# Denominators and theta in one two-bank score tile, with the key chunks around them

## The chip, the cores and the metric

The kernel runs on one core of one Trainium2 chip. Its time is that of one execution on the device in microseconds (us), the median of several runs. Engines are named as the profile does: PE (TensorE matmuls), PEld (TensorE weight loads, which can run beside matmuls), DVE (VectorE), ACT (ScalarE), POOL (GpSimd), SP (SyncE, which here only triggers transfers). Work of the core is in fp32 throughout.

## The reference

Two non-local attention layers are applied one after the other to an image batch of 4 x 128 channels x 96 x 96. Cut to what matters, a layer is:

```python
g_x     = maxpool2(conv1x1(x, g_w, g_b))        # 64 x 2304 keys: the values
theta_x = conv1x1(x, theta_w, theta_b)          # 64 x 9216 queries
phi_x   = maxpool2(conv1x1(x, phi_w, phi_b))    # 64 x 2304 keys
f = einsum('bqc,bck->bqk', theta_x, phi_x)
y = einsum('bqk,bkc->bqc', softmax(f), g_x)
out = batchnorm(conv1x1(y, W_w, W_b)) + x       # 128 channels again
```

The batch norm uses stored statistics, so it folds into the weights W and one shift.

## The kernel before

There are 8 blocks (4 images x 2 layers, `ORDER` interleaves the images so that layer 2 of one image runs after layer 1 of another). A block has 9216 queries, worked on as 9 *pairs* of 2 x 512 queries, and 2304 keys, worked on as 18 key tiles of 128.

For one pair and one key tile, `scores` (L238) writes four 64x64 matmuls into a score tile `sc` of 128 x 1024 floats, which is two PSUM banks; ACT turns it into `exp` (L244), with a constant shift in place of the row maximum, and DVE adds it into `sum` (L250). `values` (L258) multiplies `exp` with the values into `av`, which gathers over all 18 key tiles. The loop over `t` emits two key tiles of `scores`, then the two `values` of the step before: nine steps make a pair.

PSUM has three pools: `ps_sc`, two score tiles of two banks; `ps_av`, one tile of two banks; `ps_misc`, two tiles of one bank. Everything else goes through `ps_misc`:

- `denominators` (L270): a matmul of ones with `sum` of the *previous* pair; ACT copies it to `rc` (L275). `normalise` (L278 to L285, DVE) then takes the reciprocal and multiplies.
- `theta` (L227): the queries of the *next* pair; ACT adds the bias on the way out (L232).
- `pooled` (L168, a *chunk* of keys): g and phi of 384 pixels for the *next* block, of which DVE takes the 2x2 maximum into `gphi` (L172). A block needs 24 chunks, three in each of its predecessor's first eight pairs.
- `spread` (L186 to L199): after 8, 16 and 24 chunks, the phi half is centred and copied by ACT, and the g half is transposed by PE. They stand in pairs 3, 6 and 8.
- `project` (L294, L300): the output projection of the previous pair, four steps after the window.

All of these but the last stand in one place of a pair, which the text calls the *window*: after the first `values` of the pair (`j == J_WINDOW`, step 0), in the order

```python
if q: pairs[q - 1].denominators()
for step in others[:1]: step()          # chunk
if q + 1 < len(pairs): pairs[q + 1].theta()
for step in others[1:]: step()          # chunk, chunk, perhaps a spread
if q: pairs[q - 1].normalise()
```

A tile pool gives its buffers out in turn: a tile waits until the readers of the one that had its buffer before are done.

The order on PE, DVE and ACT in this loop is the order of the code: it stands inside `tc.manual_schedule(engines=...)`, where each engine named issues its instructions as written. What lies ahead of the loop is outside of it, and its order is the scheduler's: the loads of x on the queue of SP; the parameters of both layers (`load_layer`, L109 to L149), whose loads are triggered from ACT's queue; the fold of the batch norm (a square root on ACT, L135, then DVE); the transposes of the weights on PE (`transposed`, L102); all 24 chunks and three spreads of the first block; and theta of the first pair. `load_layer` triggers `var` (L133), takes the square root of it (L135) and then triggers `W_nat` (L145).

Of the kernel before, what the change touches and what calls it, by code (L numbers as in the profile page):

```python
# [9 lines left out]
F32 = mybir.dt.float32  # L10
# [6 lines left out]
P = 128  # L17
# [3 lines left out]
QT = 512  # L21
# [11 lines left out]
PT = 2 * QT  # L33
NP = HW // PT
KB = 2
NB = NKT // KB
J_WINDOW, J_PROJECT = 0, 4
# [7 lines left out]
def shifted_blocks(ctx: ExitStack, tc: tile.TileContext, x: bass.AP, layers, out: bass.AP, flag):  # L45
# [23 lines left out]
    ps_sc = ctx.enter_context(tc.tile_pool(name="ps_sc", bufs=2, space=PSUM))  # L69
    ps_av = ctx.enter_context(tc.tile_pool(name="ps_av", bufs=1, space=PSUM))  # L70
    ps_misc = ctx.enter_context(tc.tile_pool(name="ps_misc", bufs=2, space=PSUM))

    ident = const.tile([P, P], F32, name="ident")
    make_identity(nc, ident)
# [9 lines left out]
    def load_x(b):  # L84
        xt = xp.tile([C, HW], F32, tag="x", name=f"x_{b}")
        src = x[b].rearrange("c h w -> c (h w)")
        n = 6
        for i in range(n):
            nc.sync.dma_start(out=xt[:, ts(i, HW // n)], in_=src[:, ts(i, HW // n)])
        return xt  # L90
# [125 lines left out]
    class Pair:  # L216
# [4 lines left out]
            self.name = f"{blk.name}_{p}"  # L221
            self.es = {}

        def theta(self):
            ps = ps_misc.tile([P, QT], F32, tag="misc", name=f"theta_ps_{self.name}")
            for h in range(2):
                nc.tensor.matmul(  # L227
                    ps[ts(h, CI), :], lhsT=self.blk.w["theta"],
                    rhs=self.blk.xt[:, ts(2 * self.p + h, QT)], start=True, stop=True,
                )  # L230
            self.th = work.tile([P, QT], F32, tag="theta", name=f"theta_{self.name}")
            nc.scalar.activation(self.th, ps, AF.Identity, bias=self.blk.w["theta_b"])  # L232
# [31 lines left out]
                self.halves = work.tile([P, PT], F32, tag="halves", name=f"halves_{self.name}", bufs=1)  # L264
                nc.scalar.copy(self.halves, self.av)  # L265

        def denominators(self):
            ps = ps_misc.tile([P, QT], F32, tag="misc", name=f"den_ps_{self.name}")
            for h in range(2):
                nc.tensor.matmul(  # L270
                    ps[ts(h, CI), :], lhsT=ones, rhs=self.sum[:, ts(h, QT)],
                    start=True, stop=True,
                )
            self.rc = work.tile([P, QT], F32, tag="rc", name=f"rc_{self.name}", bufs=1)
            nc.scalar.copy(self.rc, ps)  # L275
# [34 lines left out]
    blocks = []  # L310
# [4 lines left out]
    def begin(n):  # L315

        b, l = ORDER[n]
        if b not in xs:
            xs[b] = load_x(b)
        blocks[n].xt = xs[b]  # L320
        blocks[n].begin_keys()

    begin(0)
    steps = blocks[0].key_steps()
# [2 lines left out]
            step()  # L327

    pairs = [Pair(blk, p, n * NP + p) for n, blk in enumerate(blocks) for p in range(NP)]
    pairs[0].theta()  # L330
    total = len(pairs) * NB
    engines = {mybir.EngineType.PE, mybir.EngineType.DVE, mybir.EngineType.Activation}
    with tc.manual_schedule(engines=engines):
        for t in range(total + NB):
            if t < total:
                q, j = divmod(t, NB)
                if q % NP == 0 and j == 0 and q // NP + 1 < len(blocks):
                    begin(q // NP + 1)
                    steps = blocks[q // NP + 1].key_steps()
                for k in range(j * KB, (j + 1) * KB):  # L340
                    pairs[q].scores(k)
            if t == 0:
                continue
            q, j = divmod(t - 1, NB)
            if j == J_PROJECT and q:
                pairs[q - 1].project()
            if t <= total:
                for k in range(j * KB, (j + 1) * KB):
                    pairs[q].values(k)
            if j == J_WINDOW:  # L350
                others = list(steps.pop(q % NP, [])) if q < len(pairs) else []
                if q:
                    pairs[q - 1].denominators()
                for step in others[:1]:
                    step()
                if q + 1 < len(pairs):
                    pairs[q + 1].theta()
                for step in others[1:]:
                    step()
                if q:  # L360
                    pairs[q - 1].normalise()

    bad = const.tile([P, 2], F32, name="bad")
    nc.vector.tensor_reduce(bad[:, 0:1], rmax, AX.X, ALU.max)
# [3 lines left out]
    ps = ps_misc.tile([P, QT], F32, tag="misc", name="bad_ps")  # L368
# [271 lines left out]
def nonlocal_blocks(tc: tile.TileContext, x: bass.AP, layers, out: bass.AP):  # L640
    with tc.tile_pool(name="flag", bufs=1) as pool:
        flag = pool.tile([1, 1], I32, name="flag")
        shifted_blocks(tc, x, layers, out, flag)
        bad = tc.nc.values_load(flag[0:1, 0:1])
        with tc.If(bad > 0):
            general_blocks(tc, x, layers, out)
# [30 lines left out]
```

## Time and profile before

| | |
|---|---|
| time, median of 3 runs | 2666.67 us (2666.65 to 2666.72) |
| span of the profiled execution | 2666.4 us |
| mean granted TensorE clock | 0.998 |
| PE busy | 2607.6 us |
| of it scores (L238) / values (L258) | 1234.2 us / 1228.8 us |
| chunks (L168) / theta (L227) / denominators (L270) / projection (L294) | 160.5 / 77.2 / 77.7 / 75.7 us |
| DVE / ACT busy | 2131.1 us / 1576.9 us |
| first chunk on PE / first scores | 29.86 us / 55.76 us |

A row of the timeline has the start in us, the duration of the merged group, the engine, the line, the operation, the tiles (output <- inputs), the shape, the count, and in brackets how long the engine was idle before and what ended that. An fp32 matmul of the code is two instructions in the trace, so `denominators` and `theta` are four each, and so is a chunk. Durations of neighbouring matmuls overlap, so the distance from one start to the next says what a group cost.

### The profile page before, as it was taken

How to read it: one execution, taken by the hardware profiler on the slowest of the kernel's cores; microseconds unless marked ns; L12 is line 12 of the kernel's file. 1: busy time of each engine (PE TensorE's matmuls, PEld its weight loads, DVE VectorE, ACT ScalarE, POOL GpSimd, SP SyncE). 2: the span in 40 equal slices, each digit the busy share in tenths (PEclk: the TensorE clock that was granted, in tenths of full speed). 3: DMA queues.
4: the chain of work that ended last, by engine and by line, in shares of the span. 5: the costliest groups of instructions: out<-in, count | busy, mean ns of one | idle time of the engine just before them, and what ended most of it. 6: DMA issues, size and time to landing. Idle time of an engine off the chain costs nothing.

```text
span 2666.4 us, 51928 instructions
## 1 busy us (share of the span) xinstructions
PE 2607.6 (98%) x22808; PEld 896.0 (34%) x22808; DVE 2131.1 (80%) x2203; ACT 1576.9 (59%) x1564; POOL 0.7 (0%) x6
## 2 busy tenths in 40 slices
PE   5999999999999999999999999999999999999998
PEld 1333333333333333333333333333333333333332
DVE  3788787888877888787888778888787887888887
ACT  2655665656656656555665666655665656666664
POOL 0000000000000000000000000000000000000000
PEclk9999999999999999999999999999999999999999
DMA  6000000000000000100000000000000000000000
GB/s 218 1 1 1 1 1 1 1 1 1 1 9 17 17 17 12 77 1 1 1 1 11 15 17 17 17 1 1 1 1 1 17 17 9 17 17 17 17 17 26
DMA packets 11690, 41.48 MB, mean 16 GB/s; under 512 B 3392, under 2 KB 3776, under 8 KB 11456
## 3 DMA queue, kind: packets, MB, share of 16 engines
q1 hardware_dynamic: 8640, 37.75, 3.6%
q8 instruction: 180, 2.95, 0.5%
q10 hardware_dynamic: 2816, 0.34, 0.1%
q14 instruction: 54, 0.44, 0.1%
HBM read 19.21 MB, written 18.87 MB: 14 GB/s over the span
## 4 chain that ended last, share of the span: by engine, by line
PE 95%; ACT 3%; DMA 1%; DVE 1%; issue 0%; ACTq 0%
PE sc L238 42%; PE av L258 41%; PE gphi_ps L168 4%; PE theta_ps L227 3%; PE den_ps L270 3%; PE W_ps L294 2%; ACT theta L232 1%; DMA W_nat<-in_L_conv_W_w_dram 0%; ACT exp L244 0%; DVE centre L186 0%; ACT phi L190 0%; DVE gphi L172 0%; ACT phi L193 0%; DMA theta_b<-in_L_conv_theta_b_dram 0%; DMA theta_nat<-in_L_conv_theta_w_dram 0%
## 5 line engine op out<-in xcount | busy, mean ns | idle before, releaser
L244 ACT ACTIVATE exp<-sc,nshift 128x1024 f32<-128x1024 f32 x1296 | 1375.0, 1112 | 805.5 <-PE sc L238 805.3
L250 DVE TENSOR_TENSOR sum<-sum,exp 128x1024 f32<-128x1024 f32 x1152 | 1410.0, 1224 | 233.1 <-ACT exp L244 142.1
L238 PE MATMUL sc<-theta,phi 64*64 64x512 f32 x10368 | 1234.2, 591 | 6.4 <-ACT exp L244 5.1
L258 PE MATMUL av<-exp,gT 64*64 64x512 f32 x10368 | 1228.8, 589 | 0.0
L258 PEld LDWEIGHTS av<-exp,gT 64*64 64x64 f32 x10368 | 396.3, 133 | 716.1 <-issue 695.0
L238 PEld LDWEIGHTS sc<-theta,phi 64*64 64x64 f32 x10368 | 387.8, 133 | 726.4 <-issue 698.2
L282 DVE RECIPROCAL rc<-rc 128x128 f32<-128x128 f32 x288 | 243.4, 907 | 0.0
L172 DVE TENSOR_REDUCE gphi<-gphi_ps 128x96 f32<-128x384 f32 x192 | 107.0, 558 | 124.2 <-PE gphi_ps L168 123.5
L248 DVE TENSOR_TENSOR sum<-exp,exp 128x1024 f32<-128x1024 f32 x72 | 88.2, 1225 | 137.7 <-ACT exp L244 137.7
L168 PE MATMUL gphi_ps<-x,gphiT 128*64 128x384 f32 x768 | 160.5, 502 | 8.9 <-DVE gphi L172 0.7
L300 DVE SCALAR_TENSOR_TENSOR x<-W_ps,shift,x 128x512 f32<-128x512 f32 x144 | 101.0, 743 | 0.5 <-PE W_ps L294 0.5
L275 ACT COPY rc<-den_ps 128x512 f32<-128x512 f32 x72 | 42.2, 587 | 98.3 <-PE den_ps L270 98.3
L265 ACT COPY halves<-av 128x1024 f32<-128x1024 f32 x72 | 72.9, 1012 | 34.4 <-PE av L258 34.4
L232 ACT ACTIVATE theta<-theta_ps,theta_b 128x512 f32<-128x512 f32 x72 | 49.5, 687 | 69.4 <-PE theta_ps L227 69.2
L168 PEld LDWEIGHTS gphi_ps<-x,gphiT 128*64 128x64 f32 x768 | 48.7, 137 | 124.1 <-ACT theta L232 45.2
L227 PE MATMUL theta_ps<-x,thetaT 128*64 128x512 f32 x288 | 77.2, 614 | 3.4 <-ACT rc L275 1.2
L294 PE MATMUL W_ps<-halves,WT 64*64 64x512 f32 x576 | 75.7, 596 | 5.0 <-DVE halves L283 5.0
L270 PE MATMUL den_ps<-sum,ones 128*64 128x512 f32 x288 | 77.7, 618 | 0.0
L283 DVE TENSOR_TENSOR halves<-halves,rc 128x512 f32<-128x512 f32 x72 | 49.8, 692 | 2.5
L280 DVE TENSOR_TENSOR halves<-halves 128x512 f32<-128x512 f32 x72 | 49.1, 682 | 1.6 <-ACT halves L265 1.6
L284 DVE TENSOR_REDUCE rmax<-rc 128x1 f32<-128x512 f32 x72 | 48.9, 678 | 0.0
L285 DVE TENSOR_REDUCE rmin<-rc 128x1 f32<-128x512 f32 x72 | 48.6, 676 | 0.0
(45 smaller groups left out, 153.8 us busy)
## 6 DMA issues: line engine op xcount, KB each, us to landing
x<-in_x_dram SPq DMA_DIRECT2D x24, 768.0 KB, 9.1
out_dram<-x SPq DMA_DIRECT2D x36, 512.0 KB, 2.6
theta_nat<-in_L_conv_theta_w_dram ACTq DMA_DIRECT2D x2, 32.0 KB, 5.2
theta_b<-in_L_conv_theta_b_dram ACTq DMA_DIRECT2D x4, 0.2 KB, 5.9
gphi_nat<-in_L_conv_g_w_dram ACTq DMA_DIRECT2D x2, 32.0 KB, 5.3
gphi_nat<-in_L_conv_phi_w_dram ACTq DMA_DIRECT2D x2, 32.0 KB, 4.9
g_b<-in_L_conv_g_b_dram ACTq DMA_DIRECT2D x2, 32.0 KB, 5.1
W_nat<-in_L_conv_W_w_dram ACTq DMA_DIRECT2D x2, 32.0 KB, 6.8
```

The costliest lines, as they stand in the source:

```text
L168: nc.tensor.matmul(ps[ts(h, CI), :CC], lhsT=self.w["gphi"][:, ts(h, CI)], rhs=self.xt[:, ts(r, CC)], start=True, stop=True,)
L172: nc.vector.tensor_reduce(self.gphi[:, ts(r, CC // 4)].rearrange("p (h w) -> p h w", w=W // 2), ps[:, :CC].rearrange("p (h a w b) -> p h w ...
L227: nc.tensor.matmul(ps[ts(h, CI), :], lhsT=self.blk.w["theta"], rhs=self.blk.xt[:, ts(2 * self.p + h, QT)], start=True, stop=True,)
L238: nc.tensor.matmul(ps[ts(c, CI), ts(h, QT)], lhsT=self.blk.phi[ts(h, CI), ts(2 * k + c, CI)], rhs=self.th[ts(h, CI), :], start=True, stop= ...
L244: nc.scalar.activation(e, ps, AF.Exp, bias=nshift)
L248: nc.vector.tensor_add(self.sum, self.es[0], e)
L250: nc.vector.tensor_add(self.sum, self.sum, e)
L258: nc.tensor.matmul(self.av[ts(h, CI), ts(r, QT)], lhsT=self.blk.gT[ts(r, CI), k, :], rhs=e[ts(r, CI), ts(h, QT)], start=(k == 0), stop=(k ...
L270: nc.tensor.matmul(ps[ts(h, CI), :], lhsT=ones, rhs=self.sum[:, ts(h, QT)], start=True, stop=True,)
L282: nc.vector.reciprocal(rc[:, ts(i, P)], rc[:, ts(i, P)])
L294: nc.tensor.matmul(pss[h][ts(c, CI), :], lhsT=self.blk.w["W"][ts(h, CI), ts(c, CI)], rhs=self.y[ts(h, CI), :], start=True, stop=True,)
L300: nc.vector.scalar_tensor_tensor(dst, pss[h], self.blk.w["shift"], dst, op0=ALU.add, op1=ALU.add)
```

## The change

Denominators and theta no longer take a bank each of `ps_misc`: they get one tile of `ps_sc`, a `room`, whose first 512 columns (one bank) are for the denominators and whose last 512 (the other) are for theta. So the room takes a turn among the score tiles, and `ps_misc` is left to chunks, transposes and projections. In the window two chunks now stand ahead of the pair of them, and the third, with the spread, behind. The point is that no two neighbours in the window should need the same bank.

The region with the written order now begins right behind the pools and holds the whole program of `shifted_blocks`, the opening too.

```diff
@@ -70,6 +70,9 @@
     ps_misc = ctx.enter_context(tc.tile_pool(name="ps_misc", bufs=2, space=PSUM))
 
+    engines = {mybir.EngineType.PE, mybir.EngineType.DVE, mybir.EngineType.Activation}
+    ctx.enter_context(tc.manual_schedule(engines=engines))
+
     ident = const.tile([P, P], F32, name="ident")
...
-        def theta(self):
-            ps = ps_misc.tile([P, QT], F32, tag="misc", name=f"theta_ps_{self.name}")
+        def theta(self, room):
+            ps = room[:, QT:]
...
-        def denominators(self):
-            ps = ps_misc.tile([P, QT], F32, tag="misc", name=f"den_ps_{self.name}")
+        def denominators(self, room):
+            ps = room[:, :QT]
...
-    pairs[0].theta()
+
+    def room(n):
+
+        return ps_sc.tile([P, PT], F32, tag="sc", name=f"den_theta_ps_{n}")
+
+    pairs[0].theta(room(0))
     total = len(pairs) * NB
-    engines = {mybir.EngineType.PE, mybir.EngineType.DVE, mybir.EngineType.Activation}
-    with tc.manual_schedule(engines=engines):
-        for t in range(total + NB):
...
-                if q:
-                    pairs[q - 1].denominators()
-                for step in others[:1]:
-                    step()
-                if q + 1 < len(pairs):
-                    pairs[q + 1].theta()
-                for step in others[1:]:
-                    step()
-                if q:
-                    pairs[q - 1].normalise()
+    for t in range(total + NB):
...
+            for step in others[:2]:
+                step()
+            both = room(q + 1)
+            if q:
+                pairs[q - 1].denominators(both)
+            if q + 1 < len(pairs):
+                pairs[q + 1].theta(both)
+            for step in others[2:]:
+                step()
+            if q:
+                pairs[q - 1].normalise()
```

## The prediction

> **What bounds the kernel now.** I read the page first: busy time by engine, then the chain that ended last.
>
> ```profile
> PE 2607.6 (98%) x22808; PEld 896.0 (34%) x22808; DVE 2131.1 (80%) x2203; ACT 1576.9 (59%) x1564; POOL 0.7 (0%) x6
> ...
> PE 95%; ACT 3%; DMA 1%; DVE 1%; issue 0%; ACTq 0%
> ```
>
> TensorE (PE) is busy 98% of the span and 95% of the chain. But a PE counted as busy may still be losing time, since matmul ends are modelled. So I took starts, not busy times, from the timeline of PE through one window (the work between two score groups of a pair).
>
> ```profile
> 205.07 1.90 PE L258 MATMUL av<-exp,gT 64*64 64x512 f32 x16
> 206.89 1.08 PE L270 MATMUL den_ps<-sum,ones 128*64 128x512 f32 x4
> 207.80 0.82 PE L168 MATMUL gphi_ps<-x,gphiT 128*64 128x384 f32 x4
> 208.66 1.08 PE L227 MATMUL theta_ps<-x,thetaT 128*64 128x512 f32 x4
> 209.57 1.82 PE L168 MATMUL gphi_ps<-x,gphiT 128*64 128x384 f32 x8
> 211.32 1.95 PE L238 MATMUL sc<-theta,phi 64*64 64x512 f32 x16
> ```
>
> Score and value groups start every 1.72 us throughout, so nothing is lost there. In the window, denominators and theta each take 0.91 to the next start (512 columns). A chunk has 384 columns, yet takes 0.86 ahead of theta, and two chunks take 1.75. What should a chunk take? The timeline of the opening, where chunks follow each other, has weight loads at 35.75, 36.40 and 37.27: 0.65 when the bank is free, 0.87 when it is not. In the first window, which has no denominators, chunk (61.93) to theta (62.63) is 0.70. So the window holds waits that no row of idle time shows. The timeline of all engines names them:
>
> ```profile
> 208.02 0.59 ACT L275 COPY rc<-den_ps 128x512 f32<-128x512 f32 x1 [1.39 <-PE den_ps L270]
> 208.66 0.20 PEld L227 LDWEIGHTS theta_ps<-x,thetaT 128*64 128x64 f32 x4 [0.71 <-ACT rc L275]
> ...
> 209.78 0.69 ACT L232 ACTIVATE theta<-theta_ps,theta_b 128x512 f32<-128x512 f32 x1 [1.18 <-PE theta_ps L227]
> ...
> 210.52 0.20 PEld L168 LDWEIGHTS gphi_ps<-x,gphiT 128*64 128x64 f32 x4 [0.81 <-ACT theta L232]
> ```
>
> Theta's weight load starts at 208.66, right after the copy of the denominators ends (208.02+0.59=208.61): third user of two banks. The third chunk's starts at 210.52, right after theta's activation ends (210.47): fifth user. The list of waits counts them:
>
> ```profile
> PEld gphi_ps L168 <- ACT theta L232: 45.2, 56, 0.8
> PEld theta_ps L227 <- ACT rc L275: 41.1, 62, 0.7
> ```
>
> 56 is 7 blocks x 8 windows with three chunks. The microseconds there are idle time of the weight loader, most of it beside running matmuls, and are not the gain.
>
> The opening matters too, because the change orders it. Its timeline:
>
> ```profile
> 19.47 0.45 ACTq L97 DMA_DIRECT2D var<-in_L_conv_bn_var_dram  x1
> ...
> 20.01 0.39 ACTq L145 DMA_DIRECT2D W_nat<-in_L_conv_W_w_dram  x1
> ...
> 27.16 0.29 ACT L135 ACTIVATE std<-var,eps 128x1 f32<-128x1 f32 x1 [12.25 <-DMA W_nat<-in_L_conv_W_w_dram]
> ...
> 29.86 9.80 PE L168 MATMUL gphi_ps<-x,gphiT 128*64 128x384 f32 x40
> ```
>
> These are layer 1's parameters. The load of W_nat is triggered *before* the square root that waits for var, although the code has it after (L135, L145). PE's first chunk follows the transpose of that W, at 29.86.
>
> **What the Trainium skill says.** "TensorE: Matmul & The Clock Gate", Part 2, step 1: matmuls stay in program order and only weight loads are pulled ahead. So a load held by a bank stops all behind it; the trace agrees (210.52). "TensorEngine Tiling (Array Packing)", Key Properties: changing the tiling mode drains the engine. The trace agrees: values to denominators is 1.82, 0.10 over 1.72, and a last chunk to scores 211.32-210.52=0.80, over the 0.65 of chunk to chunk. "PSUM — Partial Sum Buffer", Specifications, gives 512 fp32 values a bank, so a 1024-wide score tile is two banks: denominators have one half, theta the other. Its section on bank collisions asks for guards by bank, so theta's matmul need not wait for the copy of the denominators; no run shows this tile yet.
>
> **The change part by part.**
>
> *No operation is added or removed.* All durations stay; only order and buffers move.
>
> *Windows with three chunks.* New order: chunk, chunk, denominators, theta, chunk. With no wait, from the end of the values: mode change 0.10; chunk to chunk 0.65; chunk to a 512 group 0.70; denominators 0.91 (followed directly by theta in the last block, 2589.19 to 2590.10, also 0.91); theta to chunk 0.91; chunk to scores 0.80. Sum 4.07. Now: 211.32-205.07-1.72=4.53. Gain 0.46.
>
> Can it be free of waits? The third chunk takes the first chunk's bank at 206.79+3.27=210.06 on this window's clock. VectorE is busy with sums until 208.21, then needs 0.56 to reduce: free at about 208.8. The shared tile takes a score slot last read by an exp that ends before the window. The second score tile after it wants that slot back: theta's activation ends 1.81 after theta's start (208.66 to 210.47), call it 1.86 with the signal. The first score tile starts at 0.91+0.80=1.71 and the second 0.86 later, at 2.57. No wait. VectorE's third reduce comes 0.46 earlier with the window, so normalise and the projection keep their distance. Gain: 55 x 0.46 + 0.25 for the first window (3.31 now, 0.65+0.70+0.91+0.80=3.06 then) = 25.5 us.
>
> *Windows without a chunk behind theta*: 8 in the last block, 7 with the last spread. Nothing waits there now. Then the second score tile would start at theta + 0.96 + 0.86 = 1.82, and the slot is free at 1.86, with no weight load ahead. Between 0 and 0.25 each; I take 0.1: 1.5 us given back.
>
> *Spreads after chunks* (14 windows): `others[2:]` keeps them behind the last chunk, and the ScalarE work ahead of the next exp is unchanged, so the 0.7 us waits of scores on exp stay as they are.
>
> *The opening in written order.* With ScalarE ordered from the start, its queue runs W_nat of layer 0 and all of layer 1 behind the first square root (13.3). Twelve triggers then lead to var of layer 1, against eight now. Now the seventh of them (mean, 19.09) waits for the landing of the first (theta_nat, 13.45 to 19.08), six outstanding. The twelfth then waits for the sixth, triggered near 16.2: 16.2+5.5=21.7, against 19.47. Var took 7.7 to the square root (27.16): 29.4. Only now is W_nat triggered, at 29.6 in place of 20.01. It needs 4.3 (layer 0's: 9.08 to 13.3) to 9.2 (layer 1's: 20.01 to 29.2). With 0.66 to the first chunk, PE starts at 34.6 to 39.5, against 29.86. Behind that wait stand all of PE's chunks, and behind them everything. Bounds: 0, if the order of triggers does not move, and 10. The loads of x keep the DMA engines at 0.9 to 1.0 busy until 40 us, so I lean high: +7.5.
>
> Sum: 2666.7 - 25.5 + 1.5 + 7.5 = 2650.2 us.
>
> **The rivals.**
>
> A. The opening does not get longer: triggers keep their places, or W_nat lands in time. For: only the trace's order says that they were moved ahead. Against: the region names the engine whose queue triggers them. 2666.7-24.0=2642.7.
>
> B. Half the window gain is eaten by a wait I do not see, such as the third chunk on a late reduce (VectorE is 80% busy). For: sums run into the window. Against: 1.2 us of margin above. 2666.7-12.7+1.5+7.5=2663.
>
> C. The first score tile behind the window gets the shared slot. It then waits from 1.71 to 1.86 and loses its early weight load (about 0.3 in all) in 56 windows, and 1.86-0.96=0.9 in 15: +30 in place of +1.5. For: slots are not named in the code. Against: the other slot has been free longer. 2666.7-25.5+30+7.5=2679, slower.
>
> D. Theta's matmul is held behind the copy of the denominators because they share a tile: it starts 1.13+0.59+0.05=1.77 behind the denominators, not 0.91; 71 x 0.86=61. Against: dependencies are kept by region elsewhere: five transposes of gphi run at 52.49 while the last chunk's reduce still writes that tile, and only the sixth waits. 2650+61=2711, slower.
>
> **How the numbers follow.** Forecast 0.64, A 0.20, B 0.08, C 0.05, D 0.03. 0.2% is 5.3 us, so faster is under 2661.3. The forecast and A are, and a little of B: 0.87. The rest of B, and a C that nearly cancels: 0.05. C and D: 0.08. Range: A with 2 us of error gives 2640; the forecast with the opening at +10 and 0.2 us more lost in the 15 windows is 2656, and B reaches to 2662. 2640 to 2662 leaves out C and D and a tail of B.
>
> **What would show it.** Right: chunks at 0.65 to 0.70 apart, 4.07 per window, no wait of theta's load on the copy or of a chunk's on theta; chunk one near 37; W_nat's second trigger behind the second square root. Wrong: score loads waiting on theta's activation in 56 windows (C), theta 1.77 behind the denominators (D), chunk loads waiting on a reduce (B), a first chunk still at 30 (A).

## The result, and the profile after

The changed kernel takes 2701.98 us (2701.21 to 2702.55) against 2666.69 us for the kernel before on the same chip: a ratio of 1.0131, 95% interval 1.0114 to 1.0149. It is slower by 1.3%, where 0.6% faster was forecast.

The page of the changed kernel first, busy time by engine and the shares of the chain that ended last:

```profile
PE 2596.6 (96%) x22808; PEld 899.0 (33%) x22808; DVE 2122.1 (79%) x2203; ACT 1577.9 (58%) x1564; POOL 0.7 (0%) x6
...
PE 95%; ACT 3%; DMA 1%; DVE 1%; issue 0%; ACTq 0%
```

PE is busy for 11 us *less* (it was 2607.6) in a span 34 us longer: work has not grown, idle time has. The timeline of PE in the window that answers to the one shown of before:

```profile
212.15 1.90 PE L261 MATMUL av<-exp,gT 64*64 64x512 f32 x16
213.97 1.51 PE L171 MATMUL gphi_ps<-x,gphiT 128*64 128x384 f32 x8
215.31 1.03 PE L273 MATMUL den_theta_ps<-sum,ones 128*64 128x512 f32 x4
217.03 1.08 PE L230 MATMUL den_theta_ps<-x,thetaT 128*64 128x512 f32 x4 [0.69 <-ACT rc L278]
217.94 0.81 PE L171 MATMUL gphi_ps<-x,gphiT 128*64 128x384 f32 x4
218.68 1.95 PE L241 MATMUL sc<-theta,phi 64*64 64x512 f32 x16
```

and that of ACT in the same stretch:

```profile
216.39 0.59 ACT L278 COPY rc<-den_theta_ps 128x512 f32<-128x512 f32 x1 [2.68 <-PE den_theta_ps L273]
218.15 0.69 ACT L235 ACTIVATE theta<-den_theta_ps,theta_b 128x512 f32<-128x512 f32 x1 [1.18 <-PE den_theta_ps L230]
```

The chunks now run as meant: two of them in 1.34 us. But theta starts 1.72 us behind the denominators, not 0.91: it waits for the copy of the denominators, which ends at 216.39+0.59=216.98, and starts at 217.03. The list of waits (us in total, times, longest) has it 70 times, once in each of the 70 windows that hold both denominators and theta (the prediction counted 71):

```profile
PEld den_theta_ps L230 <- ACT rc L278: 109.7, 70, 1.6
...
PE den_theta_ps L230 <- ACT rc L278: 48.0, 70, 0.7
```

The waits of a chunk on theta's activation (56 before) are gone, as forecast. The opening, in its timeline:

```profile
22.99 0.44 ACTq L100 DMA_DIRECT2D var<-in_L_conv_bn_var_dram  x1
...
29.23 0.29 ACT L138 ACTIVATE std<-var,eps 128x1 f32<-128x1 f32 x1 [11.29 <-DMA var<-in_L_conv_bn_var_dram]
29.29 0.34 ACTq L148 DMA_DIRECT2D W_nat<-in_L_conv_W_w_dram  x1
...
36.45 11.16 PE L171 MATMUL gphi_ps<-x,gphiT 128*64 128x384 f32 x48
```

Layer 1's W_nat is triggered at 29.29, behind the square root that waits for var; before it was triggered at 20.01. PE's first chunk starts at 36.45 in place of 29.86.

The two profiled spans, 2666.4 and 2700.3, can be divided without a rest worth naming. The windows are taken from starts of groups in the two traces: from the start of the values to that of the first scores, less the 1.72 of the values.

| stretch | before | after | difference |
|---|---|---|---|
| start to first scores | 55.76 | 62.36 | +6.6 |
| 41 windows with three chunks and denominators | 4.54 each | 4.82 each | +11.5 |
| 14 windows with three chunks, denominators and a spread | 5.05 each | 5.33 each | +3.9 |
| 8 windows with no chunk (last block) | 1.98 each | 2.88 each | +7.3 |
| 7 windows with the last spread alone | 2.88 each | 3.40 each | +3.6 |
| the first window (no denominators) | 3.42 | 3.05 | -0.4 |
| the whole loop, first scores to last values | 2594.5 | 2620.4 | +25.9 |
| last values to the end | 16.1 | 17.5 | +1.4 |

At the end, the last store of `out` is triggered 13.05 us behind the start of the last values in both traces. But the checks of rmax and rmin, which stood ahead of the last projection's add on DVE (2657.76 and 2658.82), now stand behind it as in the code (2692.69 and 2691.36). So the flag made from them, on which the program then branches, comes 1.1 us later (14.22 behind the start of the last values, 13.11 before).

### The profile page after: what moved, and what is told of

Same layout as the page of the kernel before. It is cut to its first block, busy times and chain, and to the rows that moved or that the text cites. A ratio compares the mean times of both kernels' runs of the same rounds, so it can differ in the third digit from the quotient of the medians.

```text
span 2700.3 us, 52004 instructions
## 1 busy us (share of the span) xinstructions
PE 2596.6 (96%) x22808; PEld 899.0 (33%) x22808; DVE 2122.1 (79%) x2203; ACT 1577.9 (58%) x1564; POOL 0.7 (0%) x6
## 4 chain that ended last, share of the span: by engine, by line
PE 95%; ACT 3%; DMA 1%; DVE 1%; issue 0%; ACTq 0%
PE sc L241 41%; PE av L261 41%; PE gphi_ps L171 5%; PE den_theta_ps L230 3%; PE den_theta_ps L273 2%; PE W_ps L297 2%; ACT rc L278 2%; DMA var<-in_L_conv_bn_var_dram 1%; ACT exp L247 0%; DVE centre L189 0%; ACT phi L193 0%; PE gT_ps L199 0%; ACT phi L196 0%; DMA W_nat<-in_L_conv_W_w_dram 0%; DMA theta_b<-in_L_conv_theta_b_dram 0%
## 5 line engine op out<-in xcount | busy, mean ns | idle before, releaser
L175 DVE TENSOR_REDUCE gphi<-gphi_ps 128x96 f32<-128x384 f32 x192 | 101.5, 553 | 149.4 <-PE gphi_ps L171 148.6
L171 PE MATMUL gphi_ps<-x,gphiT 128*64 128x384 f32 x768 | 150.7, 502 | 1.2 <-DVE gT L202 0.9
L278 ACT COPY rc<-den_theta_ps 128x512 f32<-128x512 f32 x72 | 42.2, 586 | 160.2 <-PE den_theta_ps L273 159.6
L230 PE MATMUL den_theta_ps<-x,thetaT 128*64 128x512 f32 x288 | 77.6, 617 | 48.0 <-ACT rc L278 48.0
L235 ACT ACTIVATE theta<-den_theta_ps,theta_b 128x512 f32<-128x512 f32 x72 | 49.5, 687 | 85.4 <-PE den_theta_ps L230 85.4
L273 PE MATMUL den_theta_ps<-sum,ones 128*64 128x512 f32 x288 | 74.9, 598 | 0.0
L230 PEld LDWEIGHTS den_theta_ps<-x,thetaT 128*64 128x64 f32 x288 | 14.3, 134 | 110.1 <-ACT rc L278 109.7
```

What stands on the lines that cost most here:

```text
L171: nc.tensor.matmul(ps[ts(h, CI), :CC], lhsT=self.w["gphi"][:, ts(h, CI)], rhs=self.xt[:, ts(r, CC)], start=True, stop=True,)
L175: nc.vector.tensor_reduce(self.gphi[:, ts(r, CC // 4)].rearrange("p (h w) -> p h w", w=W // 2), ps[:, :CC].rearrange("p (h a w b) -> p h w ...
L230: nc.tensor.matmul(ps[ts(h, CI), :], lhsT=self.blk.w["theta"], rhs=self.blk.xt[:, ts(2 * self.p + h, QT)], start=True, stop=True,)
L273: nc.tensor.matmul(ps[ts(h, CI), :], lhsT=ones, rhs=self.sum[:, ts(h, QT)], start=True, stop=True,)
```

## The experiments

Theory 1: the framework that writes the waits into the program keeps readers and writers of a PSUM tile for the tile as a whole. The copy of the denominators is a reader of the shared tile, so theta's matmul, written behind it in the code, waits for it although it goes to the other bank. Theory 2, the rival: theta is held by something else (the chip, ScalarE's order, the turn of the score slots), and would be in any tile.

**A tile for each (two_rooms).**

```diff
-                pairs[q + 1].theta(both)
+                pairs[q + 1].theta(room(f"{q + 1}_t"))
```

> The changed kernel, but theta takes a score tile of its own and leaves the first half of it empty; order and everything else as changed. Theory 1 (the wait comes from sharing a tile: the copy of the denominators counts as a reader of the whole tile, so theta's matmul stands behind it although it writes the other bank): denominators to theta goes from 1.72 back to 0.91 us in 71 windows, 71 x 0.81 = 57.5 us less than 2702, so about 2644 to 2647, and a three-chunk window is 4.0 us. Theory 2 (theta is held by something other than the tile, such as ScalarE's order or the score slots): theta still starts 1.7 us behind the denominators and the time stays near 2702, or the second slot taken adds new waits of the scores.

Measured: 2639.01 us, ratio to before 0.9895 (0.9879 to 0.9912). PE in the window, and then ACT:

```profile
212.00 1.03 PE L273 MATMUL den_theta_ps<-sum,ones 128*64 128x512 f32 x4
212.86 1.03 PE L230 MATMUL den_theta_ps_t<-x,thetaT 128*64 128x512 f32 x4
213.72 0.81 PE L171 MATMUL gphi_ps<-x,gphiT 128*64 128x384 f32 x4
214.46 1.95 PE L241 MATMUL sc<-theta,phi 64*64 64x512 f32 x16
```

```profile
213.07 0.58 ACT L278 COPY rc<-den_theta_ps 128x512 f32<-128x512 f32 x1 [2.68 <-PE den_theta_ps L273]
213.93 0.69 ACT L235 ACTIVATE theta<-den_theta_ps_t,theta_b 128x512 f32<-128x512 f32 x1 [0.27 <-PE den_theta_ps_t L230]
```

Theta follows the denominators by 0.86 us, and the copy (213.07 to 213.65) runs while theta's matmul (from 212.86) writes the other tile. So the chip runs the two at once in different banks, which is also how the Trainium skill has it ("PSUM — Partial Sum Buffer", "PSUM bank collisions raise a hardware error"). The wait goes when the tile is no longer shared, and one line takes 63 us off. Theta now writes a bank of another score slot, so this run alone does not tell the tile from the banks; the next one keeps the banks. The expectation was 5 us too high. Each of the 70 windows gains 0.906, not 0.81: theta starts 0.855 earlier, and the group behind theta follows it 0.05 more closely once theta's weight load is not held. 70 x 0.906 = 63.4.

**The shared tile, with the copy written later (copy_behind).** The copy to `rc` moves out of `denominators` and is written between theta's matmul and its activation.

```diff
         def denominators(self, room):
...
-            self.rc = work.tile([P, QT], F32, tag="rc", name=f"rc_{self.name}", bufs=1)
-            nc.scalar.copy(self.rc, ps)
+            self.den = ps
...
-                pairs[q + 1].theta(both)
+                pairs[q + 1].theta(both, pairs[q - 1].keep_denominators if q else None)
```

> The changed kernel with the shared tile kept, but the copy of the denominators is written behind theta's matmul in the code (ahead of theta's activation). Theory 1: theta's matmul now has no earlier reader to wait for and starts 0.91 us behind the denominators; the copy in turn stands behind theta's matmul, theta's activation behind the copy, so the slot is free 2.4 us after theta's start: early enough in the windows with a chunk behind (score tile wants it at 2.5), 0.6 us late in the 15 others: 2702 - 57.5 + 9.5 = 2654. Theory 2 (hardware or slots hold theta, whatever the order of the code): 2702.

Measured: 2647.28 us, ratio 0.9925 (0.9908 to 0.9941). PE, then ACT:

```profile
213.52 1.03 PE L275 MATMUL den_theta_ps<-sum,ones 128*64 128x512 f32 x4
214.38 1.03 PE L230 MATMUL den_theta_ps<-x,thetaT 128*64 128x512 f32 x4
215.23 0.81 PE L171 MATMUL gphi_ps<-x,gphiT 128*64 128x384 f32 x4
```

```profile
215.45 0.58 ACT L283 COPY rc<-den_theta_ps 128x512 f32<-128x512 f32 x1 [3.53 <-PE den_theta_ps L230]
215.93 0.69 ACT L237 ACTIVATE theta<-den_theta_ps,theta_b 128x512 f32<-128x512 f32 x1
```

The same tile, the same banks, and no wait of theta any more: only the order in the code has changed. Theory 2 falls. And the other side of the rule shows: the copy, which needs nothing but the denominators, starts when *theta's* matmul is done, at 215.45. That is 1.93 us behind the start of the denominators, where it was 1.07 in two_rooms. Readers and writers of either half count for the tile. This way has a price: the shared slot now comes free late in the 15 windows without a chunk behind theta, whose second score tile waits for it, 0.49 us in 8 of them and 0.61 in 7. That is 8.2 us, and the time is 8.3 above two_rooms.

**The halves exchanged (swap_halves).** Theta takes `room[:, :QT]`, the denominators `room[:, QT:]`.

> The changed kernel with the halves exchanged: theta in the first bank of the shared tile, denominators in the second. If the wait belongs to the tile as a whole, theta still starts 1.72 us behind the denominators and the time stays at 2702. If it came from where the first half ends (an overlap of the two halves on one side only, or the bank that the tile starts in), it is gone: about 2640.

Measured, in a single run: 2702.47 us, and theta still waits for the copy 70 times, 48.0 us. So it is not an overlap of the halves on one side.

**The wait filled (chunk_between).** The third chunk moves between the two.

```diff
             if q:
                 pairs[q - 1].denominators(both)
+            for step in others[2:3]:
+                step()
             if q + 1 < len(pairs):
                 pairs[q + 1].theta(both)
-            for step in others[2:]:
+            for step in others[3:]:
```

> The changed kernel with its shared tile, and the third chunk moved in between denominators and theta. The copy of the denominators (done 1.72 us behind their start) then runs beside 0.91 of denominators and 0.65 of the chunk, so that theta waits only 0.16: a three-chunk window of 4.1 to 4.2 in place of 4.82, the 15 other windows as changed. 56 x 0.66 = 37 us less than 2702: 2665 +- 3. If theta's wait were not on the copy, it would grow by the chunk and the time stays near 2702.

Measured: 2660.09 us, ratio 0.9973 (0.9962 to 0.9984). PE's idle time on the copy falls from 48.0 us in 70 windows to 10.3 in the 15 that have no third chunk to put there. The wait is still there, but beside work. The two orders differ by 42 us, more than the whole change was expected to bring. The expectation had 37. In each of 55 windows 0.645 is gained, which is what a chunk takes: 35.5 us. The first window, where theta now waits for the chunk ahead, loses 0.4. The 7 us that nobody expected lie behind the seven windows with the first spread. In the changed kernel scores and values there come 0.8 and 0.2 us later than usual, because the spread's work on ACT stands ahead of the next exp (182.36 to 184.15). With the third chunk earlier, that work begins 1.0 us sooner, as seen from the scores, and the waits are gone.

**The region alone (region_only).** The kernel before, with the `manual_schedule` lines moved to the top.

> The kernel before with the written order from the top, windows and tiles as before. If the opening is the only thing that it moves, the first chunk starts at 36.5 us as in the changed kernel in place of 29.9 and the time is 2666.7 + 6.6 = 2673.3; all windows as before (4.53 us). A rival has the region change the windows too: then the sum differs by more than 2 us.

Measured: 2676.7 us, ratio 1.0034 (1.0021 to 1.0046). The loop is that of before (2594.5 us). First scores come at 60.58 (+4.8) and the end is 3.3 us longer. That is 8.1 in the profiled run and 9.3 in the medians on this chip (2667.39 before), where 6.6 was expected. A difference of over 2 us was to speak for the rival, that the region changes the windows too. The trace speaks against it: every kind of window is as long as before. W_nat is again triggered right behind the start of the square root (26.42 and 26.36), so the theory of the opening holds. The opening costs less than expected, and the end, which the expectation left out, costs more. Of its 3.3 us, 1.1 are the late flag, as in the changed kernel. The other 2.2 come behind the flag, where the program leaves: that takes 6.05 us in the kernel before, 6.3 in the changed one and 8.3 here, and what makes it vary is not shown.

**The new order without the room (order_in_misc).** The order of the change, with both tiles in the two small banks.

> The changed order (two chunks, denominators, theta, the rest) with the written order from the top, but denominators and theta in the two small banks as before: what the order does without the room. Denominators then want the first chunk's bank, whose reduce ends about 0.5 us late; theta and the third chunk find theirs nearly free. So a window of about 4.5 us, no better than before: 2671 +- 4, that is the same as region_only. If order alone were what helps, 0.46 x 56 = 26 us less: 2648.

Measured: 2677.04 us, ratio 1.0038 (1.0024 to 1.0052), the same as region_only. The weight loads of one window:

```profile
216.47 0.20 PEld L273 LDWEIGHTS den_ps<-sum,ones 128*64 128x64 f32 x4 [1.00 <-DVE gphi L175]
...
218.23 0.20 PEld L171 LDWEIGHTS gphi_ps<-x,gphiT 128*64 128x64 f32 x4 [0.71 <-ACT rc L278]
```

The wait has only moved: the denominators now wait for the first chunk's reduce. Order alone brings nothing.

**The rooms without the new order (rooms_old_order).** two_rooms, with denominators, chunk, theta, chunk, chunk as before.

> two_rooms with the order of before in the window (denominators, chunk, theta, chunk, chunk), each of denominators and theta in a score tile of its own, written order from the top. If what the change needed was only that neighbours have different banks, this order does as well: no wait in the window, 3.9 to 4.0 us, 2639 +- 3. If the order matters (the third chunk now comes two groups behind the first one and may want its bank early), the third chunk's load waits for the first chunk's reduce and the window is up to 0.3 us longer: 2650 to 2656.

Measured: 2645.84 us, ratio 0.9924 (0.9907 to 0.994). The 41 windows with three chunks and no spread are as short as in two_rooms (3.91 us); the 14 with a spread are 0.09 longer. Most of the 7 us to two_rooms is lost behind the seven windows with the last spread, where 7 x 0.91 = 6.4. The timeline of all engines in one:

```profile
354.97 0.93 ACT L193 ACTIVATE phi<-gphi,centre 64x768 f32<-64x768 f32 x1
...
355.93 0.83 ACT L196 COPY phi<-phi 64x768 f32<-64x768 f32 x1
...
356.79 0.69 ACT L235 ACTIVATE theta<-den_theta_ps_t,theta_b 128x512 f32<-128x512 f32 x1
...
357.53 1.09 PE L241 MATMUL sc<-theta,phi 64*64 64x512 f32 x8 [0.68 <-ACT theta L235]
```

The spread's copies stand ahead of theta's activation on ACT, so theta's tile, which is a score slot, comes free late. Written ahead of the denominators, as in the change, the spread delays no score tile: two_rooms has no such wait. So of the two edits to the window, buffers of their own for denominators and theta are what the chunks need, and the order is what the last spread needs.

**The opening.** trigger_first is two_rooms with the trigger of W_nat ahead of the square root:

```diff
+        W_nat = prep.tile([C, CI], F32, tag="Wnat", name=f"W_nat_{l}")
+        nc.scalar.dma_start(out=W_nat, in_=p["W_w"])
         std = const.tile([C, 1], F32, name=f"std_{l}")
         nc.scalar.activation(std, var, AF.Sqrt, bias=eps)
...
-        W_nat = prep.tile([C, CI], F32, tag="Wnat", name=f"W_nat_{l}")
-        nc.scalar.dma_start(out=W_nat, in_=p["W_w"])
```

> two_rooms, written order from the top, with the trigger of W_nat moved ahead of the square root in the code. If the wait of ScalarE's queue on var is what delays that load, it is triggered right behind var of layer 1 (23 us in place of 29) and the first chunk starts at 30 to 33 in place of 35.7: 2639 - 4.5 = 2634.5 (2633 to 2636). If the transfer itself is what takes the time, the first chunk stays near 35.7 and the time at 2639.

Measured: 2632.39 us, ratio 0.9874 (0.9857 to 0.989). Its opening:

```profile
22.52 0.33 ACTq L138 DMA_DIRECT2D W_nat<-in_L_conv_W_w_dram  x1
...
26.96 0.29 ACT L140 ACTIVATE std<-var,eps 128x1 f32<-128x1 f32 x1 [11.31 <-DMA var<-in_L_conv_bn_var_dram]
...
28.56 11.49 PE L171 MATMUL gphi_ps<-x,gphiT 128*64 128x384 f32 x48
```

Two lines of code moved give the opening back: the first chunk is at 28.56 in place of 35.74.

rooms_loop_region leaves the opening to the scheduler again, with the region around the loop alone:

> two_rooms with the written order around the loop alone, as before. Theory on the opening and end (the region costs about 6 us up to the first scores, since the load of W is triggered behind the square root, and 1.4 us at the end, since the checks of rmax and rmin are no longer ahead of the last projection): first chunk back at 30 us, 2639 - 7.5 = 2631.5, windows unchanged. Rival: the scheduler's freedom is worth nothing here and the difference between runs is the loads of x: within 2 us of 2639.

Measured: 2632.52 us, ratio 0.9878 (0.9861 to 0.9894). The time is as expected, the way is not: the scheduler starts the first scores at 41.3 among the chunks, 20.5 us earlier than two_rooms, and the stretch from there to the last values then takes 12.7 us more. The end is no shorter, though the flag is back at its old place.

Two more ask what else the opening holds. rooms_late_layer is rooms_loop_region with `load_layer(1, ...)` written behind the first block's chunks; opening_by_hand is trigger_first with layer 1's triggers behind layer 0's square root, and its square root and transposes behind the first block's chunks:

```diff
+    w0, prepare = load_layer(0, layers[0])
+    prepare()
+    w1, prepare = load_layer(1, layers[1])
...
     for n in sorted(steps):
         for step in steps[n]:
             step()
+    prepare()
```

> rooms_loop_region with layer 1's parameters loaded and prepared behind the first block's chunks in the code. If PE's first chunk waits only for the last weight transpose ahead of it, it now starts behind layer 0's, near 17 us, and x's first part has landed by then: 13 us less, about 2618. If the chunks then wait for x (loads of x keep the transfer engines busy until 40 us), a good part is lost: 2622 to 2628.

> trigger_first with layer 1's loads triggered behind layer 0's square root, and its square root and transposes written behind the first block's chunks. The first chunk then starts behind layer 0's transposes, near 17 us in place of 28.6, and the first scores near 43.5 in place of 54.8; the loop as in two_rooms. 2632.4 - 10.5 = 2622. If the chunks run into the loads of x, 2625 to 2630.

Measured: 2625.19 us (ratio 0.9844, 0.9828 to 0.9861) and 2625.38 us (0.984, 0.9824 to 0.9856). These are the fastest of all the runs. First chunks start at 16.3 and 18.0, but both gain less than that, and not because chunks wait for x, as the second half of each expectation had it. In rooms_late_layer a chunk waits 3.53 us (until 28.88) for a reduce, and on DVE that reduce stands behind layer 1's fold of the batch norm, which waits for its square root until 28.00. In opening_by_hand layer 1's transposes hold PE from 41.3 to 44.6 ahead of theta, and the first scores come at 47.3 in place of 43.5.

## Why the prediction was wrong

The step that failed is the line "denominators 0.91 (followed directly by theta in the last block ...)" and with it the paragraph "Can it be free of waits?". It asked for the bank, the slot and the queue, and never for the tile: it went from what the chip's banks need to what the framework writes. The runs show in its place that theta waits for the copy of the denominators, so that it starts 1.71 us behind them where 0.91 was forecast (0.86 in two_rooms). The prediction did write the case down as rival D, priced at 71 x 0.86 = 61 us, and gave it 3 in 100. The mechanism of D is what the runs show, and its price is close: 70 windows, not 71, with 0.855 at theta and 0.05 behind it, 63.4 in all. D's whole time, 2711, is 9 us too high, because the rest of the windows came out shorter than reckoned.

The evidence against D was that five of the six transposes of gphi run while a reduce still writes gphi. The observation stands, but gphi is a tile in SBUF. It was carried to a PSUM tile that no row of the trace covered, and there it does not hold. A rule about waits was taken from one memory to the other without a run. That the memory is what makes the difference is likely but not shown: these are two tiles, one of each kind.

The other steps:

- The waits in the windows with three chunks were read rightly. two_rooms, which removes them without making the new one, has windows of 3.91 us where 4.07 was worked out and 4.54 measured before. The terms of denominators, theta and the last chunk were 0.05 too large each. They were taken from places where a weight load had been held or had started only with its group (denominators straight behind values in the last block, both at 2589.19), and that costs the group 0.05 more.
- The third chunk finds its bank free and scores find the slot free, as worked out: in two_rooms PE waits for neither in these windows. The list of waits does have the sign that was named for C, 58 waits of score loads on theta's activation, in the changed kernel too. But there the activation has ended (218.84) before the load starts (219.16), at the usual 0.28 behind the last one, so nothing is lost. Rivals B and C did not happen.
- The 15 windows without a chunk behind theta were to give back 0.1 each, since "nothing waits there now". With a tile for each, the 8 in the last block stay at 1.98, and the 7 with the last spread gain: 2.88 to 2.49. Something did wait in those 7, and the prediction's own list had it: 62 waits of theta's load on the copy are 55 with three chunks and these 7.
- The opening was right in mechanism and near in size: +7.5 was forecast, +6.6 to the first scores and +1.4 at the end were measured, and trigger_first shows the cause. Within the chain, var of layer 1 was triggered at 22.99 where 21.7 was worked out, and took 6.2 us to the square root where 7.7 was taken, so that two misses all but cancelled (29.23, for 29.4). The end was not thought of. Rival A fell.

Without D's wait the time is that of two_rooms, 2639.0, just below the range that began at 2640. So there is a second, smaller error, in the terms of the windows: with D's wait gone they gain 37.5 us, where 24.0 was forecast. The large error is one wait, in the place where the change was meant to remove one.

What stays open: the opening of kernels with the same written order varies, first chunks from 34.9 to 36.5 us. In all of them the first chunk comes 0.68 us behind the landing of layer 1's W_nat (34.18 in region_only, 35.77 in the changed kernel), but why the loads land earlier or later the runs don't say. PE writing one bank of a tile while ACT reads the other bank of the *same* tile was not tried, since the program always has a wait there.

## What to carry to other kernels

In these runs a two-bank PSUM tile was the unit of waiting as well as of space. Two values that are written and read at different times then want two tiles, even where one tile has a bank for each, or the copies must be written behind both matmuls, which cost 8 us here. Before a wait is called gone, ask what the tool that writes the waits knows, and get that from a run of the same memory and not of another. When a written order is spread over more of a program, look for triggers of transfers that stood ahead of a wait only because a scheduler had put them there.

## What the runs showed of the hardware

A weight load that had to wait costs more than the wait. A 512-column group whose load was held takes 0.909 us to the next start, and one whose load was free takes 0.858 (theta to chunk, changed kernel and two_rooms). A last chunk before scores takes 0.745 in the changed kernel, where its load was free, against 0.80 in the kernel before, where it was held. Of the 0.906 us that each window gained in two_rooms, 0.05 is this.

A matmul into one bank and ScalarE's copy out of another ran at the same time in two_rooms (213.07 to 213.65), at no cost: theta took the same 0.858 us as in the first window, which has no copy.
